# Where the matrices stand in the load queue: behind the first slot's four samples instead of ahead of all samples

## The chip, the cores and the metric

One core of one Trainium2 chip. The metric is device time in microseconds, as the median of several runs of the whole kernel; the profile shows one execution. A core has the engines PE (TensorE, matmul), DVE (VectorE), ACT (ScalarE), POOL (GpSimd) and SP (SyncE), and 16 DMA engines that move data between HBM and the on-chip memory (SBUF). PE writes into a memory of its own (PSUM).

## The reference

```python
def setup_inputs():
    x            # (128, 128, 1024) float32: B samples of C x T
    itok_B_0_7   # (128,) int32, 0..7: which subject a sample belongs to
    L0_cond_weights  # (8, 128, 128) float32: a C x D matrix for each subject

def reference(x, itok_B_0_7, L0_cond_weights):
    w = L0_cond_weights[itok_B_0_7]
    return x + jnp.einsum('bct,bcd->bdt', x, w)
```

Each of the 128 samples is multiplied by its subject's matrix, and the sample itself is added. A sample is 512 KB, and so are the eight matrices together; 67.1 MB of samples are read and as many written.

## The kernel before

**Tiling.** Four samples make a slot, `xs[k]`, of shape 128 partitions x 4 x 1024 (2 MB); there are 12 slots and 32 turns. A slot has two halves of two samples each, and a half is the unit of compute (64 of them, `j`). Results are added in place, so a slot is loaded, computed on, stored, and loaded again.

**SP** issues all loads on one queue: first the eight matrices into `w_all` (L161), then 128 loads of one sample each (issued in the helper `transfer`, L57, called from `load`). A load of `xs` into SBUF takes a sample as 32 rows of 16 KB on the HBM side; the matrices are rearranged from `s c d` to `c s d`, so that one contiguous piece is 512 B. From turn 12 on, SP waits before the loads until the slot's stores have landed.

**ACT** loads the subject numbers at the start (L141) and issues all stores (L57): the first slot in two halves of 1 MB, later slots whole, 2 MB. Its queue is a different one from SP's, but both are served by the same 16 DMA engines.

**DVE** clears `zeros`, works out the index from the subject numbers (L153 to L157), and does one addition for each half (L217): PSUM plus `xs`, into `xs`.

**POOL** reads 16 indices at a time into registers (L185) and copies each sample's matrix out of `w_all` into one of four small buffers `w` (L196). Before the first copy it waits for the matrices (`s_wall`). For halves 0 and 1 the copies do not wait for samples; from half 2 on, they wait for the addition two halves before and for the half's first sample.

**PE** runs three products on zeros at the start (L146), then for each half four products of 512 columns (L206), two for a sample, each split into two passes. For halves 0 and 1 it waits first for the samples and then for POOL's copies; from half 2 on, for the copies alone.

So the order in time at the start is: matrices and samples arrive, POOL copies, PE multiplies, DVE adds, ACT stores.

Of the kernel before, what the change touches and what calls it, by code (L numbers as in the profile page):

```python
# [41 lines left out]
DMA = 16  # L42
# [7 lines left out]
def transfer(nc, engine, out, in_):  # L50

    later, nc._always_lower_symbolic_ap = nc._always_lower_symbolic_ap, False
    ins, outs = engine.lower_ap_dma(in_), engine.lower_ap_dma(out)
    nc._always_lower_symbolic_ap = later
    return engine.add_instruction(  # L57
        mybir.InstDMACopy(
            name=nc.get_next_instruction_name(),
            engine=engine.engine,  # L60
            ins=ins,
            outs=outs,
            mode="Copy",
            cce_op=ALU.bypass,
            queue=QUEUES[engine.engine],
        )
    )


@with_exitstack  # L70
def kernel(
    ctx: ExitStack,
    tc: tile.TileContext,
    x: bass.AP,
    subjects: bass.AP,
    weights: bass.AP,
    out: bass.AP,
):
    nc = tc.nc
    B, C, T = x.shape  # L80
    S, _, D = weights.shape
    NT = B // (G * H)

    def sbuf(name, *shape, dtype=F32):
        return ctx.enter_context(nc.sbuf_tensor(name, list(shape), dtype)).ap()

    given, near, wrap, index = (
        sbuf(name, 1, B, dtype=I32) for name in ("given", "near", "wrap", "index")
    )
    w_all = sbuf("w_all", C, S, D)  # L90
    ws = [sbuf(f"w{i}", C, 1, D) for i in range(W_SLOTS)]
    zeros = sbuf("zeros", C, N)
    xs = [sbuf(f"x{i}", C, H * G, T) for i in range(SLOTS)]
    ps = [
        ctx.enter_context(nc.psum_tensor(f"ps{i}", [D, G, T], F32)).ap() for i in range(P_SLOTS)
    ]

    s_given = tc.alloc_semaphore("s_given")
    s_wall = tc.alloc_semaphore("s_wall")
    s_index = tc.alloc_semaphore("s_index")  # L100
    s_zeros = tc.alloc_semaphore("s_zeros")
    s_copied = tc.alloc_semaphore("s_copied")
    s_product = tc.alloc_semaphore("s_product")
    s_added = tc.alloc_semaphore("s_added")

    s_pair = [[tc.alloc_semaphore(f"s_pair{i}_{h}") for h in range(H)] for i in range(SLOTS)]


    s_first = tc.alloc_semaphore("s_first")

    def emptied(i, h):

        turns = i // SLOTS
        return (DMA * G + (DMA if h == H - 1 else 0)) * turns

    def loaded(i, q):

        h = q // G
        return s_pair[i % SLOTS][h], emptied(i, h) + DMA * G

    def load(engine, i, q):
        k, h = i % SLOTS, q // G
        transfer(
            nc,
            engine,
            xs[k][:, q, :],
            x[i * H * G + q].rearrange("(a r) t -> a (r t)", r=ROWS),
        ).then_inc(s_pair[k][h], DMA)

    def store(i, q0, q1):  # L130
        k, b = i % SLOTS, i * H * G
        transfer(
            nc,
            nc.scalar,
            out[b + q0 : b + q1].rearrange("g d t -> d g t"),
            xs[k][:, q0:q1, :].rearrange("d (o g) t -> d o (g t)", g=min(G, q1 - q0)),
        ).then_inc(s_first if i == 0 and q1 == G else s_pair[k][(q1 - 1) // G], DMA)

    with tc.tile_critical():  # L139

        nc.scalar.dma_start(given, subjects.rearrange("(o b) -> o b", o=1)).then_inc(s_given, DMA)  # L141

        nc.vector.memset(zeros, 0.0).then_inc(s_zeros, 1)  # L143
        nc.tensor.wait_ge(s_zeros, 1)
        for _ in range(IDLE):
            nc.tensor.matmul(  # L146
                ps[P_SLOTS - 1][:, G - 1, :N], zeros[:, :D], zeros, start=True, stop=True
            )

        nc.vector.wait_ge(s_given, DMA)
        nc.vector.tensor_scalar(near, given, -S, S - 1, ALU.max, ALU.min).then_inc(s_index, 1)  # L153
        nc.vector.wait_ge(s_index, 1)
        nc.vector.tensor_scalar(wrap, near, 0, S, ALU.is_lt, ALU.mult).then_inc(s_index, 1)  # L155
        nc.vector.wait_ge(s_index, 2)
        nc.vector.tensor_tensor(index, near, wrap, ALU.add).then_inc(s_index, 1)  # L157
        nc.gpsimd.wait_ge(s_index, 3)


        nc.sync.dma_start(w_all, weights.rearrange("s c d -> c s d")).then_inc(s_wall, DMA)  # L161
        for i in range(NT):
            k = i % SLOTS
            if i == SLOTS:
                nc.sync.wait_ge(s_first, DMA)
            if i >= SLOTS:
                nc.sync.wait_ge(s_pair[k][H - 1], emptied(i, H - 1))
            for q in range(H * G):
                load(nc.sync, i, q)


        for j in range(NT * H):
            i, q0, q1 = j // H, j % H * G, (j % H + 1) * G
            k = i % SLOTS
            p = ps[j % P_SLOTS]

            ahead = j < P_SLOTS
            if ahead:  # L180
                nc.tensor.wait_ge(*loaded(i, q0))
            for q in range(q0, q1):
                b = i * H * G + q
                if b % R == 0:
                    _, subject = nc.values_load_multi_w_load_instructions(  # L185
                        index[0:1, b : b + R],
                        engines=[mybir.EngineType.Pool],
                        min_val=0,
                        max_val=S - 1,
                        skip_runtime_bounds_check_because="the index is clamped on the chip above",  # L190
                    )
                if b == 0:
                    nc.gpsimd.wait_ge(s_wall, DMA)
                if not ahead and q == q0:
                    nc.gpsimd.wait_ge(s_added, j - P_SLOTS + 1)
                copy = nc.gpsimd.tensor_copy(  # L196
                    ws[b % W_SLOTS], w_all[:, bass.ds(subject[b % R], 1), :]
                )
                if not ahead and q == q0:
                    copy.wait_op(*loaded(i, q0), "sem-ge")  # L200
            copy.then_inc(s_copied, 1)

            nc.tensor.wait_ge(s_copied, j + 1)
            for q in range(q0, q1):
                for t in range(0, T, N):
                    mm = nc.tensor.matmul(  # L206
                        p[:, q % G, t : t + N],
                        ws[(i * H * G + q) % W_SLOTS][:, 0, :],
                        xs[k][:, q, t : t + N],
                        start=True,  # L210
                        stop=True,
                    )
            mm.then_inc(s_product, 1)

            mine = xs[k][:, q0:q1, :]
            nc.vector.wait_ge(s_product, j + 1)
            nc.vector.tensor_tensor(  # L217
                mine, p, mine, ALU.add
            ).then_inc(s_added, 1)

            if i == 0 or q1 == H * G or i == NT - 1:
                nc.scalar.wait_ge(s_added, j + 1)
                store(i, q0 if i in (0, NT - 1) else 0, q1 - (b == B - 1))

    with tc.tile_critical() as waits:
        for i in range(NT - SLOTS, NT):
            nc.sync.wait_ge(s_pair[i % SLOTS][H - 1], emptied(i + SLOTS, H - 1))
        nc.sync.wait_ge(s_pair[(NT - 1) % SLOTS][0], emptied(NT - 1 + SLOTS, 0) + DMA)  # L230
    last = nc.scalar.dma_start(out[B - 1], xs[(NT - 1) % SLOTS][:, H * G - 1, :])

    tc.add_manual_dep(
        last.ins,
        waits.name,
        mybir.DependencyInfo(mybir.DependencyClass.NoSync, mybir.DependencyReason.SCHED_ONLY),
        reason="the end of the program waits for it",
    )
# [27 lines left out]
```

## Time and profile before

| what | value |
|---|---|
| median of 3 runs | 327.0 us (326.23 to 327.02) |
| profiled execution: span | 325.4 us |
| PE busy | 241.1 us (74%) |
| DVE busy | 147.9 us (45%) |
| POOL busy | 34.3 us (11%) |
| load queue (q1), share of 16 DMA engines | 49.7% |
| store queue (q10), share of 16 DMA engines | 49.1% |
| matrices, from issue to landing | 4.5 us |
| a sample, from issue to landing (median) | 32.3 us |
| a store of 2 MB, from issue to landing (median) | 47.3 us |

The span runs from the first to the last thing in the profiled execution; the device time also has what lies around it. The two queues' shares add up to 98.8%: the DMA engines are occupied nearly from end to end. "From issue to landing" contains the time in the queue, so a large number there means a full queue, not a slow transfer.

### The profile page before, as it was taken

The page shows a single profiled execution, that of the slowest core. Times are in us where ns is not written, and L with a number is a line of the kernel's source. Part 1 is how long each engine was busy: PE and PEld are TensorE (multiplying, and loading weights), DVE is VectorE, ACT ScalarE, POOL GpSimd, SP SyncE. Part 2 cuts the span into 40 slices and gives each one's busy share as a digit, 9 for nine tenths or more (in the row PEclk, how much of TensorE's full clock was granted, in tenths as well). Part 3 has the DMA queues.
Part 4 walks back from the last instruction along what each step waited for, and adds up shares of the span by engine and source line. Part 5 has one row for each costly group of instructions (what it writes and reads, how often), then busy time and mean ns, then how long its engine had stood idle before and what let it go on. Part 6 is the DMA issues. An engine that isn't in the chain of part 4 may idle for free.

```text
span 325.4 us, 1606 instructions
## 1 busy us (share of the span) xinstructions
PE 241.1 (74%) x518; PEld 95.2 (29%) x518; DVE 147.9 (45%) x68; POOL 34.3 (11%) x132
## 2 busy tenths in 40 slices
PE   6999988988888888888888888888888689000000
PEld 2444332333333333333333333333333233000000
DVE  1375754555555555454555555554554544200000
POOL 1011111011111111111011111111111010000000
PEclk9999999999999999999999999999999889655555
DMA  6999999999999999999999999999999999999994
GB/s 250 413 418 421 428 425 422 420 428 427 426 421 427 429 415 427 424 431 423 423 435 417 416 432 424 428 417 428 433 419 424 418 437 415 429 425 427 426 428 201
DMA packets 16074, 134.85 MB, mean 414 GB/s; under 512 B 2625, under 2 KB 3650, under 8 KB 3906
## 3 DMA queue, kind: packets, MB, share of 16 engines
q1 hardware_dynamic: 7184, 67.64, 49.7%
q10 hardware_dynamic: 8882, 67.11, 49.1%
q8 instruction: 4, 0.07, 0.1%
q14 instruction: 4, 0.03, 0.0%
HBM read 67.63 MB, written 67.11 MB: 414 GB/s over the span
## 4 chain that ended last, share of the span: by engine, by line
PE 42%; DVE 20%; issue 16%; POOL 4%; DMA 2%; POOLq 1%; SPq 0%
PE ps L206 42%; DVE x L217 20%; POOL w L196 4%; DMA x<-in_x_dram 2%; POOLq L196 1%; SPq L57 0%; SPq L161 0%; POOLq L139 0%; SPq L262 0%; SPq L139 0%
## 5 line engine op out<-in xcount | busy, mean ns | idle before, releaser
L206 PE MATMUL ps<-x,w 128*128 128x512 f32 x512 | 236.1, 607 | 33.6 <-POOL w L196 32.1
L217 DVE TENSOR_TENSOR x<-ps,x 128x2048 f32<-128x2048 f32 x64 | 146.7, 2292 | 129.1 <-PE ps L206 129.1
L206 PEld LDWEIGHTS ps<-x,w 128*128 128x128 f32 x512 | 93.3, 191 | 176.6 <-issue 93.9
L196 POOL COPY w<-w_all 128x128 f32 x128 | 34.1, 296 | 238.0 <-DMA x<-in_x_dram 207.7
L146 PE MATMUL ps<-zeros 128*128 128x512 f32 x6 | 5.0, 992 | 1.7 <-DVE zeros L143 1.7
L146 PEld LDWEIGHTS ps<-zeros 128*128 128x128 f32 x6 | 1.8, 328 | 3.7 <-issue 2.1
L143 DVE MEMSET zeros<- 128x512 f32 x1 | 0.5, 485 | 1.1 <-SPq L139 1.1
L153 DVE TENSOR_SCALAR near<-given 1x128 int32<-1x128 int32 x1 | 0.2, 215 | 0.6 <-DMA given<-in_itok_B_dram 0.6
L157 DVE CUSTOM_DVE_ANT_0 index<-near,wrap 1x256 uint16<-1x256 uint16 x1 | 0.3, 278 | 0.0
L155 DVE TENSOR_SCALAR wrap<-near 1x128 int32<-1x128 int32 x1 | 0.2, 216 | 0.0
L253 POOL MEMSET const-float32-0.0<- 128x1 f32 x1 | 0.1, 99 | 0.2 <-issue 0.2
L253 POOL MEMSET const-bfloat16-1.0<- 128x1 bf16 x1 | 0.1, 102 | 0.0
L253 POOL MEMSET const-uint8-127<- 128x1 uint8 x1 | 0.1, 102 | 0.0
L253 POOL MEMSET const-float32-1.0<- 128x1 f32 x1 | 0.1, 99 | 0.0
## 6 DMA issues: line engine op xcount, KB each, us to landing
x<-in_x_dram SPq DMA_DIRECT2D x128, 512.0 KB, 32.3
out_dram<-x ACTq DMA_DIRECT2D x30, 2048.0 KB, 47.3
out_dram<-x ACTq DMA_DIRECT2D x3, 1024.0 KB, 13.9
out_dram<-x ACTq DMA_DIRECT2D x2, 512.0 KB, 21.1
w_all<-in_L_cond_weights_dram SPq DMA_DIRECT2D x1, 512.0 KB, 4.5
given<-in_itok_B_dram ACTq DMA_DIRECT2D x1, 0.5 KB
```

The lines of the kernel that those rows point to most:

```text
L143: nc.vector.memset(zeros, 0.0).then_inc(s_zeros, 1)
L146: nc.tensor.matmul(ps[P_SLOTS - 1][:, G - 1, :N], zeros[:, :D], zeros, start=True, stop=True)
L153: nc.vector.tensor_scalar(near, given, -S, S - 1, ALU.max, ALU.min).then_inc(s_index, 1)
L155: nc.vector.tensor_scalar(wrap, near, 0, S, ALU.is_lt, ALU.mult).then_inc(s_index, 1)
L157: nc.vector.tensor_tensor(index, near, wrap, ALU.add).then_inc(s_index, 1)
L196: copy = nc.gpsimd.tensor_copy(ws[b % W_SLOTS], w_all[:, bass.ds(subject[b % R], 1), :])
L206: mm = nc.tensor.matmul(p[:, q % G, t : t + N], ws[(i * H * G + q) % W_SLOTS][:, 0, :], xs[k][:, q, t : t + N], start=True, stop=True,)
L217: nc.vector.tensor_tensor(mine, p, mine, ALU.add).then_inc(s_added, 1)
L253: nc = _bacc.Bacc("TRN2", target_bir_lowering=False, num_devices=1)
```

## The change

The load of the matrices, one issue on SP, is moved from ahead of the loop over the slots to behind the four loads of the first slot. Its queue, its shape and its semaphore stay; so does everything on the other engines.

```diff
         nc.gpsimd.wait_ge(s_index, 3)
 
 
-        nc.sync.dma_start(w_all, weights.rearrange("s c d -> c s d")).then_inc(s_wall, DMA)
         for i in range(NT):
             k = i % SLOTS
             if i == SLOTS:
...
                 nc.sync.wait_ge(s_pair[k][H - 1], emptied(i, H - 1))
             for q in range(H * G):
                 load(nc.sync, i, q)
+            if i == 0:
+                nc.sync.dma_start(w_all, weights.rearrange("s c d -> c s d")).then_inc(s_wall, DMA)
```

## The prediction

> **What bounds the kernel now.** I read the page first (its slices and byte counts), then the timeline of the first microseconds, then tables of short stretches at the start, in the middle and at the end.
>
> The page:
>
> ```profile
> span 325.4 us, 1606 instructions
> ...
> PEclk9999999999999999999999999999999889655555
> DMA  6999999999999999999999999999999999999994
> GB/s 250 413 418 421 428 425 422 420 428 427 426 421 427 429 415 427 424 431 423 423 435 417 416 432 424 428 417 428 433 419 424 418 437 415 429 425 427 426 428 201
> ...
> HBM read 67.63 MB, written 67.11 MB: 414 GB/s over the span
> ```
>
> The DMA row is 9 in every slice but the first and the last. The chain of waits credits PE with 42%, but PE, DVE and POOL finish at 278.7 us, and from there to 324.4 us only stores run. So the end is the moment when 16 DMA engines have moved 134.85 MB. A change counts only if it alters the time before the stream starts, the speed of the stream, or the unevenness of its end. The first slice (8.1 us) moved 250 GB/s where the others move 413 to 437; there something is lost.
>
> The timeline of the first 24 us (start, duration, engine, line):
>
> ```profile
> 0.96 0.43 SPq L161 DMA_DIRECT2D w_all<-in_L_cond_weights_dram  x1
> 1.46 23.51 SPq L57 DMA_DIRECT2D x<-in_x_dram  x28
> ...
> 1.67 4.96 PE L146 MATMUL ps<-zeros 128*128 128x512 f32 x6 [1.67 <-DVE zeros L143]
> ...
> 5.58 1.00 POOL L196 COPY w<-w_all 128x128 f32 x4 [5.13 <-DMA w_all<-in_L_cond_weights_dram]
> ...
> 8.18 16.15 PE L206 MATMUL ps<-x,w 128*128 128x512 f32 x37 [1.54 <-DMA x<-in_x_dram]
> ...
> 14.24 3.99 ACTq L57 DMA_DIRECT2D out_dram<-x  x2
> ```
>
> Here the matrices are issued at 0.96 us, the samples queue behind them, POOL copies as soon as the matrices land, and PE starts only when sample 1 is in. The first store is issued at 14.24 us; the DMA records have its first packet at 18.54 us.
>
> Stretches while the matrices arrive (busy times by engine, then the granted clock, DMA share and GB/s):
>
> ```profile
> 2.00:2.50 0.50, 0.50 (x1) 0.17 (x1) 0.29 (x2) 0.00 (x0) 1.00 0.69 79
> 2.50:3.00 0.50, 0.50 (x2) 0.32 (x1) 0.42 (x2) 0.00 (x0) 1.00 0.21 63
> 3.00:3.50 0.50, 0.50 (x1) 0.02 (x1) 0.00 (x0) 0.00 (x0) 1.00 0.76 227
> 3.50:4.00 0.50, 0.50 (x2) 0.34 (x1) 0.00 (x0) 0.00 (x0) 1.00 1.00 303
> ```
>
> The matrices' packets (1024 of 512 B in the records, the first at 2.07 us) ramp up slowly and reach 303 GB/s only at 3.5 us. Then loads alone, loads with stores, and stores alone:
>
> ```profile
> 9.00:14.00 5.00, 5.00 (x13) 2.23 (x12) 2.09 (x1) 0.00 (x0) 1.00 0.99 403
> 20.00:66.00 46.00, 41.90 (x95) 17.13 (x94) 27.21 (x13) 6.41 (x24) 1.00 1.01 425
> 280.00:315.00 35.00, 0.00 (x0) 0.00 (x0) 0.00 (x0) 0.00 (x0) 0.50 1.01 426
> ```
>
> Loads alone are about 5% slower than the mixed stream. Last, a place where PE had stood idle for 2.4 us and comes back at 258.4 us:
>
> ```profile
> 255.00:258.50 3.50, 1.11 (x4) 0.28 (x3) 2.29 (x1) 0.53 (x2) 1.00 1.02 431
> 258.50:262.00 3.50, 3.50 (x5) 1.44 (x6) 0.00 (x0) 0.00 (x0) 0.51 1.01 426
> ```
>
> The clock falls to 0.51 and 3.5 us hold 5 matmuls, where 8 fit at full clock.
>
> **The change, part by part.** The compiled order on the SP queue is as the diff says: four x issues, the matrices, then 124 x issues. The other engines keep their instructions. Nothing is added.
>
> *Taken from the head: 2.55 us.* By 3.5 us the matrices have moved (79 + 63 + 227) x 0.5 us = 0.185 MB of 0.524 MB; the rest at 303 GB/s takes 1.12 us, so the mean engine ends them at 4.62 us. From 2.07 that is 2.55 us; the records show each engine's first x packet between 4.13 and 4.95 us, which agrees.
>
> *Put back behind sample 3: 1.73 us.* 0.524 MB at 303 GB/s, with no ramp. In the new place the matrices are issued at 0.96 + 4 x 0.636 (the spacing of x issues: 594 ns and a gap) = 3.5 us; from issue to first packet took 1.1 us, so they are ready by 4.6 us, and their turn comes only at 7.4 us. Lower bound: at the 403 GB/s of loads alone, 1.30 us. Upper bound: the whole 2.55 us, if the ramp is the matrices' own (first touches, say) and comes with them. I take 1.73, since the ramp consists of engines with nothing to do, and in mid-queue they have samples ahead of it.
>
> [...]
>
> *A ramp of the samples at the head: 0.2 us.* No row shows x going first. Lower bound 0: a sample is two 16 KB packets for each engine, 1.28 us of work, and the next issue follows after 0.64 us, so no engine runs dry. Upper bound: the 0.82 us (2.55 - 1.73) that the matrices' ramp took. The one long first x packet (1.40 us where the other fifteen took 0.61 to 0.63) points the same way: 0.79 us if all did that. Being one in sixteen, it puts the value near the lower end.
>
> *The compute starts later, and loads alone last longer: 0.2 us.* Samples stream from 2.3 us; four at 1.28 us (the spacing of their landings in the records) bring us to 7.4, the matrices to 9.1; from the mean end of the matrices to POOL's first copy it took 5.58 - 4.62 = 0.96 us, so POOL starts at 10.1 us, and with two copies (0.53) and the handover (0.06) PE at 10.65, 2.5 us later than now. PE is then idle from 6.63 to 10.65 us, 4.0 us, longer than the 2.4 us after which its clock was 0.51. There, four matmuls came at 0.86 us spacing instead of 0.43, so 1.7 us more (0 if the clock stays). Behind PE wait DVE's first add, ACT's first store, and POOL, which needs the add for its next copies. All of these come 2.5 to 4.2 us later, first store issue near 18.4 us. The cover is the load queue, which has 48 samples (12 slots) to run before it needs a store: sample 48 was issued at 66.6 us, and the two stores of slot 0 that it waits for had landed by 31.5 us. That margin of 35 us is eight times the delay, so no load waits. The price is only that loads alone, at 403 and not 425 GB/s, last 4.2 + 2.35 - 1.73 = 4.8 us longer (the start is 2.35 earlier, 1.73 of it is matrices): 4.8 x 5% = 0.24, 0.15 if the clock stays. I take 0.2. PE, with 3.43 us a half-slot against about 4.3 us that the mixed stream needs to bring one, catches up by about 60 us instead of 39.
>
> [...]
>
> *Sum:* -2.55 + 1.73 + 0.2 + 0.2 = -0.42 us. On the profiled execution that is 325.4 to 325.0 us; 1.6 us lie between this span and the median of 327.0, unchanged. So 326.6 us. Lower ends together: -2.55 + 1.30 + 0 + 0.15 = -1.10, 325.9; upper ends: -2.55 + 2.55 + 0.82 + 0.24 = +1.06, 328.1.
>
> **Rivals.** *Faster, 325.9 us.* The end belongs to one engine: the last store landed between 320.6 and 324.4 us over the 16 engines, the last 1.9 us after the second last. If that one began its samples at 4.95 us rather than at the mean, it wins 0.33 us more; with no ramp of x and the block at 1.30 us the gain passes 1 us. For it: x packets never showed a general ramp. Against it: 303 GB/s is a steady row, and early lags of 0.37 us stayed with engines other than the last.
>
> *Slower, 328.0 us.* The ramp belongs to cold starts, not to a place. The samples pay it at the head (0.82) and the matrices pay it again at theirs (2.55 in all): +1.06 us with the longer stretch of loads. It decides from a total ramp of about 1.7 us. For it: single 512 B packets of 0.70 to 1.00 us at 2.1 to 2.3 us, in four engines. Against it: fifteen first x packets without a delay.
>
> *Nothing, 327.0 us.* The last engine's lag grows from 0.4 us at 24 us to 3.1 us past the median engine at the end; it may have its own cause and close the small gain again.
>
> *The change does not do what it says:* excluded by the queue's order.
>
> **How the numbers follow.** A measurement of this kernel can tell about 0.3%, 1.0 us, from no change. The forecast (a gain of 0.1 to 0.9 us) gets 0.50, nothing 0.10, faster 0.26, slower 0.14. So faster by over 0.3%: 0.26; within: 0.60; slower: 0.14. The time is the forecast's, 326.6 us. The range runs over the bounds, with 0.2 us more below, since the three runs spread over 0.8 us: 325.7 to 328.1.
>
> **What would show it.** Right: over 380 GB/s by 3 us; POOL's first copy near 10.1 us, PE's first product near 10.65 at half clock for some 3 us, first store issue near 18; every middle slice of DMA still 9; a span of 325.0 us. The ramp of x is wrong if 2.1 to 3.0 us again shows under 200 GB/s; the cost of the block is wrong if POOL starts after 10.9 us; a dip of the DMA row around 60 to 70 us would mean that late stores do hold up loads, which would break the whole argument.

## The result and the profile after

| | before | after |
|---|---|---|
| median of 8 runs each | 326.53 us (326.23 to 327.21) | 327.41 us (327.27 to 327.69) |
| ratio after / before | | 1.0023, 95% interval 1.0014 to 1.0032 |
| span of the profiled execution | 325.4 us | 325.6 us |

The kernel became slower by 0.14 to 0.32%, where 326.6 us and a gain were forecast. The time lies within the stated range, but on the other side of no change, and partly by luck: the forecast started from a median of 327.0 us (3 runs), which 8 runs put at 326.53. Counted from there, a gain of 0.42 us was forecast and a loss of 0.88 us came. The two profiled spans differ by only 0.2 us, because the profiled execution of before seems to have been one of its slower ones: the changed kernel's profiled run took 327.36 us for its span of 325.6, and with the same 1.8 us around it the span of before makes 327.2, against a median of 326.5.

The page of the changed kernel:

```profile
span 325.6 us, 1606 instructions
...
PEclk9599999999999999999999999999999879755555
DMA  7999999999999999999999999999999999999995
GB/s 244 387 412 418 428 427 421 426 423 426 427 427 425 429 421 420 431 421 427 425 424 428 417 428 423 428 425 430 426 420 425 434 421 420 429 424 430 424 430 226
```

The DMA engines are still full from the second slice on; no dip stands near 60 to 70 us, so the late stores left no gap in the stream. But the first two slices moved 244 and 387 GB/s, where they moved 250 and 413 before. The clock falls in the second slice.

Its timeline (start, duration, engine, line):

```profile
0.97 2.46 SPq L57 DMA_DIRECT2D x<-in_x_dram  x4
...
3.47 0.59 SPq L170 DMA_DIRECT2D w_all<-in_L_cond_weights_dram  x1
...
11.56 0.99 POOL L197 COPY w<-w_all 128x128 f32 x4 [11.11 <-DMA w_all<-in_L_cond_weights_dram]
...
12.23 14.14 PE L207 MATMUL ps<-x,w 128*128 128x512 f32 x29 [6.12 <-POOL w L197]
...
19.71 4.01 ACTq L57 DMA_DIRECT2D out_dram<-x  x2
```

The order is as intended. POOL starts at 11.56 us where 10.1 was forecast: the matrices came late. Stretches of its start (busy times of PE, PEld, DVE and POOL, then granted clock, DMA share, GB/s):

```profile
2.00:3.00 1.00, 1.00 (x2) 0.48 (x2) 0.71 (x3) 0.00 (x0) 1.00 0.95 262
3.00:4.00 1.00, 1.00 (x2) 0.36 (x2) 0.00 (x0) 0.00 (x0) 1.00 0.84 344
4.00:5.00 1.00, 1.00 (x2) 0.34 (x1) 0.00 (x0) 0.00 (x0) 1.00 1.06 410
5.00:6.00 1.00, 1.00 (x3) 0.19 (x1) 0.00 (x0) 0.00 (x0) 1.00 1.22 295
6.00:7.00 1.00, 0.11 (x1) 0.00 (x0) 0.00 (x0) 0.00 (x0) 1.00 0.60 229
7.00:8.00 1.00, 0.00 (x0) 0.00 (x0) 0.00 (x0) 0.00 (x0) 1.00 1.12 426
8.00:9.00 1.00, 0.00 (x0) 0.00 (x0) 0.00 (x0) 0.00 (x0) 0.67 0.58 209
9.00:10.00 1.00, 0.00 (x0) 0.00 (x0) 0.00 (x0) 0.00 (x0) 0.50 1.17 350
```

and the same two stretches of the kernel before, which has samples in its queue there as well:

```profile
5.00:6.00 1.00, 1.00 (x2) 0.34 (x1) 0.00 (x0) 0.42 (x2) 1.00 0.83 344
6.00:7.00 1.00, 0.63 (x2) 0.00 (x0) 0.00 (x0) 0.59 (x3) 1.00 0.85 344
```

A packet counts in the stretch where it starts, so a single row is coarse; over 5 to 7 us it is 262 against 344 GB/s. The stream of samples has a slow spot there. (From 8.26 us on the matrices' own packets of 512 B run: 280 GB/s over 8 to 10 us.) The DMA records say it sharper. The landing of a transfer, as the median over the 16 engines:

| landing, us | before | after |
|---|---|---|
| sample 0 | 6.34 | 4.39 |
| sample 1 | 7.75 | 5.67 |
| sample 2 | 9.03 | 7.77 |
| sample 3 | 10.31 | 9.15 |
| matrices | 5.03 (first) | 10.94 |
| sample 4 | 11.59 | 12.23 |
| last store | 321.28 | 322.14 |

When sample 4 lands, both kernels have moved the same bytes: the changed one is 0.64 us behind. At the last store, again the median over the engines, it is 0.86 us behind. That is close to the difference of the two times (0.88), but it comes from one profile each, and in these two the end itself, which the last engine sets (324.42 and 324.59 us), differs by 0.17 us only: in the profile of before the last engine lagged more. In between, sample 2 lands 2.10 us behind sample 1, where the samples behind the matrices land 1.28 us apart; and packets of 16 KB that start in the slow spot take up to 1.81 us, where those between 11 and 16 us take 0.61 to 0.65. The engines are not idle there: their share over 5 to 7 us is 0.91, the mean of the two rows.

Later stretches of the changed kernel, mixed stream and stores alone:

```profile
20.00:66.00 46.00, 46.00 (x108) 20.06 (x107) 30.08 (x14) 7.27 (x28) 1.00 1.01 423
280.00:315.00 35.00, 0.00 (x0) 0.00 (x0) 0.00 (x0) 0.00 (x0) 0.52 1.01 427
```

Against 425 and 426 before, the stream itself has not changed; the 423 contain the last 4 us of loads alone (the first store's packets start at 23.76 us).

### The profile page after: what moved, and what is told of

Its sections match the earlier page's. It is cut to its first block, busy times and chain, and to the rows that moved or that the text cites. A ratio compares the mean times of both kernels' runs of the same rounds, so it can differ in the third digit from the quotient of the medians.

```text
span 325.6 us, 1606 instructions
## 1 busy us (share of the span) xinstructions
PE 240.0 (74%) x518; PEld 96.6 (30%) x518; DVE 147.9 (45%) x68; POOL 34.0 (10%) x132
## 3 DMA queue, kind: packets, MB, share of 16 engines
q1 hardware_dynamic: 7184, 67.64, 49.9%
q10 hardware_dynamic: 8882, 67.11, 49.1%
## 4 chain that ended last, share of the span: by engine, by line
PE 48%; DVE 16%; issue 14%; POOL 4%; DMA 2%; SPq 1%; POOLq 1%
PE ps L207 48%; DVE x L218 16%; POOL w L197 4%; DMA w_all<-in_L_cond_weights_dram 2%; SPq L57 1%; POOLq L197 1%; SPq L263 0%; SPq L139 0%
## 5 line engine op out<-in xcount | busy, mean ns | idle before, releaser
L207 PEld LDWEIGHTS ps<-x,w 128*128 128x128 f32 x512 | 94.9, 192 | 175.1 <-issue 102.2
```

Of the source, the lines that this page charges most:

```text
L207: mm = nc.tensor.matmul(p[:, q % G, t : t + N], ws[(i * H * G + q) % W_SLOTS][:, 0, :], xs[k][:, q, t : t + N], start=True, stop=True,)
```

## The experiments

Two readings of the slow spot were open: (A) the matrices' many small packets, prepared behind sample 3, disturb the samples ahead of them; (B) samples that go first have the slow spot by themselves. A third explanation of the loss is the later start of the compute. All ratios are to the kernel before; runs 1, 4, 5 and 12 are edits of the kernel before, the others of the changed kernel.

**1. The samples alone.**

```diff
+        nc.vector.memset(w_all, 0.0).then_inc(s_wall, 1)
         nc.gpsimd.wait_ge(s_index, 3)
...
-        nc.sync.dma_start(w_all, weights.rearrange("s c d -> c s d")).then_inc(s_wall, DMA)
...
-                    nc.gpsimd.wait_ge(s_wall, DMA)
+                    nc.gpsimd.wait_ge(s_wall, 1)
```

> Leaves out the load of the matrices (zeros are written into their buffer instead, so the products are zero). Theory A: the slow spot of the changed kernel at 5.3 to 7 us (sample 2 lands 2.10 us after sample 1 instead of 1.28 us) is caused by the matrices' 1024 small packets being prepared behind it. Then without them samples 2 and 3 land 1.28 us apart, the stretch 5 to 7 us moves about 400 GB/s, and the kernel takes about 324.5 us (0.994 of before): 0.52 MB less at 303 GB/s, the slow spot of 0.82 us gone, and stores starting some 6 us earlier than in the changed kernel. Theory B: the slow spot belongs to the first samples of a queue, whatever stands behind them. Then 5 to 7 us stays near 260 GB/s and the time is about 325.3 us (0.996). Both: the first samples' packets still take 0.8 to 1.15 us.

325.84 us, ratio 0.9976 (0.9967 to 0.9985). Its stretches:

```profile
4.00:5.00 1.00, 1.00 (x2) 0.34 (x1) 0.04 (x1) 0.55 (x3) 1.00 0.87 311
5.00:6.00 1.00, 1.00 (x2) 0.34 (x1) 0.00 (x0) 0.46 (x2) 1.00 1.47 262
6.00:7.00 1.00, 1.00 (x2) 0.00 (x0) 0.00 (x0) 0.00 (x0) 1.00 0.56 213
7.00:8.00 1.00, 0.91 (x3) 0.51 (x3) 0.00 (x0) 0.00 (x0) 1.00 0.84 344
```

The slow spot is there without any matrices (238 GB/s over 5 to 7 us; sample 2 lands 2.26 us behind sample 1). Theory A falls, B stands, though the time came out 0.5 us above B's 325.3. And 0.52 MB less, 1.73 us at the matrices' own 303 GB/s, saved only 0.5 to 1.1 us against the kernel before (sample 4 lands at 10.66 instead of 11.59 us): at the head of this queue the matrices cost less than their transfer. The reading is that their ramp stands where the samples' larger one would be.

**2. The matrices behind eight samples** (`if i == 1` instead of `if i == 0`).

> The matrices stand behind eight samples instead of four. Theory A: the slow spot moves with them, to about 7.9 to 9.6 us, and sample 2 lands 1.28 us after sample 1. Theory B: it stays at 5.3 to 7 us. Under both the compute starts 5.1 us later than in the changed kernel, and loads alone last that much longer, at 5% a microsecond: 327.7 us (1.003 of before). If late compute were dearer than that (the whole 0.88 us for 4.05 us of delay), 328.5 us (1.006).

328.05 us, 1.0042 (1.0028 to 1.0055). Sample 2 again lands 2.10 us behind sample 1: the spot stays with the samples. The first store is issued at 26.26 us, 6.6 us later than in the changed kernel, for about 0.6 us of time: 0.1 us a microsecond if all of it were due to that, though the two intervals overlap.

**3. The matrices in rows of 16 KB.**

```diff
-                nc.sync.dma_start(w_all, weights.rearrange("s c d -> c s d")).then_inc(s_wall, DMA)
+                transfer(
+                    nc,
+                    nc.sync,
+                    w_all.rearrange("c s d -> c (s d)"),
+                    weights.rearrange("s (a r) d -> (s a) (r d)", r=32),
+                ).then_inc(s_wall, DMA)
```

> Same place as in the changed kernel, behind four samples, but the same 0.52 MB are read in rows of 16 KB as a sample is, so that the matrices lie in another order and the products are of other matrices. Theory A (the number of small packets): no slow spot, the block takes 1.28 us instead of 1.79 us, time about 326.0 us (0.9985 of before). Theory B: slow spot stays, only the block is shorter: 326.9 us (1.001). A third, that the first touch of the matrices' memory slows the stream whatever its packets are: like B in time, but with the slow spot inside or right behind the block.

327.08 us, 1.0018 (1.0009 to 1.0027). The block lands 1.42 us behind sample 3 instead of 1.79, as B expected. Sample 2 comes 1.62 us behind sample 1 in the median, and six of the 16 engines lie some 1.1 us behind the other ten: the slow spot is there, but it fell on a part of the engines.

**4. Late compute alone**, in the kernel before:

```diff
                     nc.gpsimd.wait_ge(s_wall, DMA)
+                    nc.gpsimd.wait_ge(*loaded(1, 0))
```

> The kernel before, with the matrices ahead of all, but POOL's first copy also waits for samples 4 and 5: the DMA stream's head is unchanged and only the compute starts later (PE near 13.9 us instead of 8.2, first store some 7 us later with the slow clock). It prices the late compute alone. My sum: loads alone last 7 us longer at 5%: +0.35 us, 326.9 us (1.0011 of before). Rival: the late compute is the whole loss of the changed kernel (0.88 us for a first store 5.47 us later): +1.1 to 1.2 us, 327.7 us (1.0035).

326.64 us, 1.0004 (0.9995 to 1.0013). Its timeline:

```profile
13.81 1.00 POOL L197 COPY w<-w_all 128x128 f32 x4 [13.36 <-DMA x<-in_x_dram]
...
14.48 11.97 PE L207 MATMUL ps<-x,w 128*128 128x512 f32 x23 [8.54 <-POOL w L197]
...
22.38 3.99 ACTq L57 DMA_DIRECT2D out_dram<-x  x2
```

The first store leaves at 22.4 instead of 14.2 us, later even than in the changed kernel, and the time rises by at most 0.42 us (the end of the interval; by 0.13 at its middle). That leaves room for the 5% a microsecond of the sum, does not show it, and excludes late compute as the whole cause.

**5. The matrices on the store queue**, behind the subject numbers.

```diff
         nc.scalar.dma_start(given, subjects.rearrange("(o b) -> o b", o=1)).then_inc(s_given, DMA)
+        nc.scalar.dma_start(w_all, weights.rearrange("s c d -> c s d")).then_inc(s_wall, DMA)
...
-        nc.sync.dma_start(w_all, weights.rearrange("s c d -> c s d")).then_inc(s_wall, DMA)
```

> The matrices go to the store queue, right behind the 0.5 KB of subject numbers, and the samples start on their own queue at once. If the DMA engines share their time between the two queues by bytes, the matrices land at about 6 us, the compute starts near 7 us and the time is about 326.6 us (1.000 of before): the samples' ramp is paid, the late compute is not. If they share it by packets, a 512 B packet stands behind each 16 KB packet, 64 of them on each engine, and the matrices land only after some 64 x 0.64 = 41 us; stores then start near 50 us instead of 18.5, and loads alone last 30 us longer at 5%: +1.5 us, about 328.7 us with the ramp (1.0065).

326.45 us, 0.9990 (0.9980 to 0.9999). The 512 B packets did not alternate one by one with the 16 KB ones here: the matrices land at 8.30 us, neither 6 nor 41. Some 900 of their 1024 packets start between 3.8 and 5.5 us, and from 4.0 to 5.0 us no 16 KB packet of a sample starts.

```profile
5.00:6.00 1.00, 1.00 (x3) 0.19 (x1) 0.00 (x0) 0.00 (x0) 1.00 1.18 422
6.00:7.00 1.00, 0.06 (x1) 0.00 (x0) 0.00 (x0) 0.00 (x0) 1.00 1.11 449
7.00:8.00 1.00, 0.00 (x0) 0.00 (x0) 0.00 (x0) 0.00 (x0) 1.00 0.94 386
```

Here 5 to 7 us moves 436 GB/s, although the samples start first: no slow spot. Sample 4 lands at 11.25 us. The first store leaves at 18.38 us, near the 19.71 of the changed kernel, and yet the time is not above that of before: with the slow spot gone, the loss is gone too.

**6. A small read ahead of the samples** (64 KB of sample 0 into an unused buffer, then the changed kernel).

> The changed kernel with a read of 64 KB (128 pieces of 512 B of sample 0, into a buffer of its own that nothing uses) ahead of the samples. If the ramp of the samples is a start cost that any first transfer takes upon itself, the first 16 KB packets take 0.61 to 0.65 us and sample 2 lands 1.28 us behind sample 1: about 326.2 us (0.9988 of before). If the slow spot at sample 2 belongs to large packets on a fresh queue, only the first packets get faster and sample 2 is late as before: about 327.2 us (1.002).

327.85 us, 1.0038 (1.0023 to 1.0052). Nothing is taken over: the first sample's packets still take 0.64 to 1.07 us, and sample 2 lands 2.24 us behind sample 1, although it is now the fourth transfer of the queue and not the third. The time is 0.65 us above even the second expectation; the small read itself puts the first packet of a sample from 2.31 to 2.84 us.

**7. The whole stream held back by 2 us** (`nc.sync.wait_ge(s_index, 3)` ahead of the loads).

> The changed kernel, but SP issues nothing until the index is ready, so the whole stream starts 2.0 us later. If the slow spot comes at a time of its own (5.3 to 7 us after the start, from something beside the kernel), it stays there and hits sample 1 instead of sample 2. If it belongs to the queue's third sample, it moves to 7.3 to 9 us. The time is about 329.4 us under both, less by 0.5 us if the first packets are fast.

328.96 us in one run.

```profile
6.00:7.00 1.00, 0.44 (x2) 0.00 (x0) 0.00 (x0) 0.00 (x0) 1.00 1.16 442
7.00:8.00 1.00, 0.00 (x0) 0.00 (x0) 0.00 (x0) 0.00 (x0) 1.00 0.90 262
8.00:9.00 1.00, 0.00 (x0) 0.00 (x0) 0.00 (x0) 0.00 (x0) 1.00 1.04 377
```

The slow spot moves with the stream, to 7 to 8 us, and is again at sample 2, but smaller (1.63 us behind sample 1). From the first issue to the landing of sample 0 it takes 3.47 us, against 3.42: the slow first packets belong to the stream's start too.

**8. Shorter rows for the first four samples** (4 KB instead of 16 KB).

> The changed kernel with the first four samples read in rows of 4 KB instead of 16 KB (128 rows a sample instead of 32). If large packets make the ramp, it goes: sample 2 lands 1.3 us behind sample 1 and the time is about 326.6 us (1.000 of before). If not, it stays: 327.4 us (1.0027).

327.44 us, 1.0028 (1.0018 to 1.0038). Sample 2 lands 2.29 us behind sample 1: the length of the rows, 4 or 16 KB, is not the cause.

**9. Another order of the first four** (`for q in (2, 3, 0, 1) if i == 0 else range(H * G)`).

> The changed kernel, but the first slot's samples are loaded in the order 2, 3, 0, 1. If the slow spot belongs to a place in the queue, the third transfer, now sample 0, is late: about 2.1 us behind the second. If it belongs to the memory that sample 2 lies in, sample 2, now first, takes it on top of the first packets, and the third transfer follows in 1.28 us. Time about 327.4 us under both, as the compute waits for the matrices anyway.

327.47 us in one run. The third transfer, now sample 0, lands 2.11 us behind the second, and the first as before at 4.39 us. The spot belongs to the place in the queue, or to a time after the stream's start, not to the memory that is read. No run holds place and time apart.

**10 and 11. The matrices behind one sample, and behind two** (the issue inside the loop over `q`, after `q == 0` or after `q == 1` of slot 0).

> The matrices stand behind one sample. Their packets then run where the slow spot was, before the third transfer. If the slow spot falls upon the third transfer whatever it is, sample 1 lands 2.1 us behind the matrices, PE starts near 8.9 us and the time is about 327.0 us (1.001 of before). If matrices ahead of the third transfer spare it, as they do in the kernel before, only the first packets' 0.5 us is paid: PE starts near 8.1 us, about 326.2 us (0.999).

> The matrices stand behind two samples and are themselves the third transfer. If the slow spot falls upon the third transfer or comes 3 us after the stream's start, it now lies in the matrices, which land 2.6 us behind sample 1 (1.75 + 0.85), near 8.3 us; PE starts near 9.5 us and the time is about 327.2 us (1.002). If the small packets hide it, they land 1.75 us behind sample 1, near 7.5 us, and the time is about 326.5 us (1.000).

Behind one: 327.38 us, 1.0027 (1.0017 to 1.0036); the matrices land 1.73 us behind sample 0 with no slow spot, and sample 1, now third, 1.77 us behind them, 0.49 late. Behind two: 327.02 us, 1.0018 (1.0008 to 1.0029); the matrices, now third, land 1.80 us behind sample 1 and show no slow spot in that profile. So neither expectation of a pair held fully: a sample as third transfer was late, the matrices were not.

Run 10 also separates the two explanations of the loss, since its compute starts almost as early as that of before:

```profile
6.72 1.00 POOL L197 COPY w<-w_all 128x128 f32 x4 [6.26 <-DMA w_all<-in_L_cond_weights_dram]
...
14.63 10.92 ACTq L57 DMA_DIRECT2D out_dram<-x  x3
```

The first store leaves at 14.63 us, against 14.24 before, and the kernel is 0.88 us slower all the same (0.0027 x 326.5).

**12. The matrices on the store queue, ahead of the subject numbers.**

> The matrices on the store queue, now ahead of the subject numbers, so issued at 0.9 us instead of 1.5 us; the samples start at once on their own queue. The ramp of both queues overlaps and the matrices land about 0.6 us earlier than in the run where they stood behind the subject numbers (median landing 8.3 us), so the compute starts that much earlier: 326.3 us (0.9987 of before). If the matrices' landing is set by their alternation with the samples' packets and not by their issue, it stays at 8.3 us and 326.45 us (0.999).

326.55 us, 1.0002 (0.9993 to 1.0011). The matrices land at 6.22 us, 2.1 us earlier than in run 5, but POOL starts only at 8.36 us (9.01 in run 5): the subject numbers, now behind, let DVE begin the index at 6.09 us instead of 2.18, and from its end at 6.86 it takes POOL another 1.5 us to start. No gain over run 5 can be told.

Taken together, with sample 4 and the matrices both through (the landing of sample 4, one profile each) beside the ratio:

| kernel | landing, us | ratio |
|---|---|---|
| on the store queue, run 5 | 11.25 | 0.9990 |
| late compute alone, run 4 | 11.34 | 1.0004 |
| on the store queue, run 12 | 11.35 | 1.0002 |
| rows of 16 KB, run 3 (six engines about 1 us later) | 11.54 | 1.0018 |
| behind two | 11.57 | 1.0018 |
| before | 11.59 | 1 |
| behind one | 11.90 | 1.0027 |
| another order, run 9 (one run) | 12.16 | 1.0029 |
| changed kernel | 12.23 | 1.0023 |
| short rows | 12.31 | 1.0028 |
| small read first (64 KB more) | 12.80 | 1.0038 |
| held back by 2 us, run 7 (one run) | 13.77 | 1.0069 |

The later the head is through, the slower the kernel: a straight line through the twelve gives 0.9 us of time for each microsecond of landing (0.3% is 1 us), and a kernel lies up to 0.35 us off it. Behind one, behind two and run 3 lie 0.3 us above the line; what they lose beyond their landing is not explained. Before and run 4 have the same head and land 0.25 us apart, which is the size of one profile's scatter.

## Why the prediction was wrong

**What bounds the kernel** was right: full DMA engines until the end (the two queues take 49.9% and 49.1% of the 16 engines' span), and a change that counts only through the head of the stream.

**Taken from the head, 2.55 us**: nearly right. The samples' packets start from 2.31 us on instead of 4.13 to 4.95, but the 2.55 are counted from 2.07 us, where the matrices' packets started. The prediction says itself that samples stream from 2.3 us; the 0.24 us between are in no term of its sum and are counted with the ramp below.

**Put back, 1.73 us**: right, 1.79 measured. The lower bound of 1.30 us, the rate of the 16 KB packets, was not reached: in the same place 16 KB rows took 1.42 us (run 3) and 512 B pieces 1.79. The sign set for this step, POOL after 10.9 us, came up (11.56), but through the ramp and not through the block.

**A ramp of the samples at the head, 0.2 us with an upper bound of 0.82**: this step failed. Without a ramp sample 0 would land 1.77 us after the stream's first packet at 2.07 (that is what it took before, from a mean start of 4.57 to 6.34), so at 3.84 us, and sample 3 at 3.84 + 3 x 1.28 = 7.68 us. It landed at 9.15: the ramp is 1.47 us, of which 0.55 lies in sample 0 (0.24 of it the later first packet), 0.82 in the slow spot at sample 2 and 0.10 at sample 3. I had argued that one long first packet in sixteen put the value low, and took the matrices' ramp as the upper bound. Both rested on a stream that another transfer had opened; no row of before showed samples opening it, and a bound borrowed from a different transfer was no bound. Run 1 shows that the ramp is the samples' own (sample 2 2.26 us behind sample 1 without any matrices), run 9 that it does not belong to the memory read (2.11 us with another sample in third place). My sign for it, under 200 GB/s from 2.1 to 3.0 us, was also set wrong: the row of 2 to 3 us has 262, and the spot came later. The sign for a right forecast, over 380 GB/s by 3 us, did fail (344 from 3 to 4 us).

**Compute later, 0.2 us**: the steps before it shifted it (PE at 12.23 instead of 10.65 us, first store at 19.71 instead of 18.4), its price is not contradicted: run 4 gives at most 0.42 us for a delay of 8.1 us, and from sample 4 to the last store the changed kernel loses 0.86 - 0.64 = 0.22 us, no more than the scatter of one profile. Of the 5% that loads alone are slower, a part came from a coarse row: a sample every 1.28 us is 410 GB/s and not 403, which makes 3.6% against 425. PE caught up later than forecast, at 76 us instead of about 60 (its row of 20 to 66 us is busy throughout). The DMA row stayed at 9, so no wait for a store opened a gap in the stream. PE did come back at half clock, as the two rows say:

```profile
12.00:14.00 2.00, 1.77 (x2) 0.84 (x3) 0.00 (x0) 0.56 (x3) 0.50 0.98 401
14.00:16.00 2.00, 2.00 (x5) 0.94 (x4) 0.00 (x0) 0.00 (x0) 0.71 1.01 410
```

The clock's record falls to half at 8.34 us, 2.2 us after PE's last product on zeros (it ended at 6.11 us), and comes back at 15.16. In the kernel before it falls at 258.55 us, 2.6 us after the end of the last product ahead of the pause (255.98 us; PE was back at 258.37).

**The sum with what was measured**: -2.55 + 1.79 + 1.47 + 0.22, less 0.13 that sample 1 loses before (1.41 us behind sample 0 instead of 1.28) and no longer does, is +0.80 us. The medians give +0.88. The agreement is closer than the terms deserve: each is read from one profile, and with the landing of run 4 (11.34 us) in place of that of before the head alone would have lost 0.89 us.

**The rivals.** The slower one had the right side and nearly the price (1.06 us), but not the mechanism: the matrices did not pay their ramp again (1.79 us, where 2.55 were taken from the head); the samples alone paid almost the whole. "From a total ramp of about 1.7 us" was sound as a threshold of 0.3%, and 1.47 is just below it. For the faster one nothing was found. The last engine's lag behind the median one was 2.45 us against 3.14, so the unevenness of the end does not explain the loss; in these two profiles it hides most of it.

**Open** is what slows the third sample. It is not the matrices (run 1: 2.26 us behind the second), not the memory read (run 9: 2.11), not the length of the rows (run 8: 2.29), not a time apart from the stream's start (run 7, where it moved with the stream), and 64 KB ahead did not spare it (run 6: 2.24). The matrices at the head of the queue (sample 2 1.28 us behind sample 1), or beside it on the other queue (436 GB/s over 5 to 7 us), did; behind one sample they left 0.49 us of it. One thing goes with it in the traces: in the changed kernel and in runs 2, 6, 7, 8 and 9 one issue of a load on SP, begun between 4.7 and 6.9 us, takes 0.90 to 1.52 us, where the other issues of the first 15 us take about 0.6 (0.56 to 0.65 in the changed kernel; 0.81 at most in runs 1 and 3); in before and in runs 4, 5, 10, 11 and 12 no early issue takes over 0.70. The load so delayed in the changed kernel, sample 5, is issued from 4.78 to 5.83 us and lands at 13.51, so the long issue did not leave the queue empty; whether the two have one cause is not shown. Slower issuing of the loads, and a first transfer of between 64 and 512 KB, were not tried.

## What to carry to other kernels

In these profiles what opens the DMA stream pays a start cost, and that cost depends on what opens it (0.82 us for the matrices, 1.47 for the samples): leaving out the matrices, 1.73 us of transfer, saved only 0.5 to 1.1 us (run 1), and the reading is that they spared the samples' larger ramp. In this kernel, with its DMA engines 99% occupied, moving the matrices behind one, two or four samples bought nothing (ratios 1.0027, 1.0018 and 1.0023): the head did not get measurably shorter (sample 4 lands at 11.90, 11.57 and 12.23 us, against 11.59 before). So, in a kernel whose stream is as full as this one's, measure the stream without the moved transfer before pricing its place. A cost that no row shows is not bounded by another transfer's row: the bound of 0.82 us met a ramp of 1.47.

## What the runs showed of the hardware that was not expected

The third sample of the load queue lands 2.1 to 2.3 us behind the second in six of the profiles with no matrices ahead of it (the changed kernel and runs 1, 2, 6, 8 and 9; in runs 3 and 7 the median engine shows 1.62 and 1.63), and in the changed kernel some packets take up to 1.81 us there instead of the 0.61 to 0.65 of later ones, with the engines 91% at work; a few transfers later the spacing is 1.28 us again. And in run 5 the 512 B packets on the store queue did not take turns one by one with the 16 KB packets on the load queue: the matrices landed at 8.30 us beside samples, where turn by turn an estimate gave 41.
